# Wide fp32 products of TensorE made as four quarter-width products side by side, in a cross-attention kernel

## The chip, the cores and the metric

The kernel runs on one core of a Trainium2 chip. The metric is the device time of one execution in microseconds (us). The core's engines run side by side, each with a queue of its own: TensorE (PE in the profile, its weight loads PEld) multiplies, VectorE (DVE) and ScalarE (ACT) do elementwise work and reductions, GpSimd (POOL) does some of that too, and SyncE (SP) issues the transfers between the core's memory and HBM.

## The reference

A cross-attention layer with a second, "adapter" attention, all in fp32, over x of 2 batches, 2048 rows and 640 columns, and a context of 2 x 128 rows and 384 columns. The last 4 context rows (`ca`) feed the adapter, the other 124 (`enc`) the text attention:

```python
query = hidden_states @ Wq
keyt = enc @ Wk
valt = enc @ Wv
hs = _mha(query, keyt, valt)                     # 8 heads of 80 columns
ca_q1 = jnp.einsum('btc,th->bch', ca, Wq_ca)[:, indices, :]
ca_hs1 = _mha(ca_q1, residual, residual)         # 2048 x 2048, with 384 distinct rows
ca_q2 = ca_hs1 @ Wq
ca_hs2 = _mha(ca_q2, ca @ Wk_ca, ca @ Wv_ca)
out = (hs + ca_hs2) @ Wout + b_out
out = out + residual
```

## The kernel before, in words

**Products.** A product has a stationary operand `lhsT` (rows x columns), loaded into TensorE as weights, and a moving operand `rhs` with the same rows; the result has as many partitions as `lhsT` has columns. Every fp32 product gives two weight loads and two matmul records in the trace. A product of 128 rows by 128 columns fills TensorE's array ("wide" below). Smaller ones fill a part of it, and several that lie in different parts stand side by side: the profile writes `128*32` for 128 rows by 32 columns (a "strip"), `64*128` and `32*128` for products that fill some of the rows. The wide ones are the query projection (`pq`, from x turned, `xt`, and Wq; for six of the eight blocks of 512 rows in a form with fewer products and sums of x and Wq, `queries_fast`), the output projection (`po`, from the hidden states `hs` and Wout, also with sums; and `po2` with `w2_sb`), and in the setup `pk`, `pv`, `pw`, `pa`. Products that were already strips are `ph` (`hidden`: probabilities `pT` by the values `vpad`, 16 units of 24 products) and `acc` (`contract`: the adapter's `ea` by `y_sb`). The text scores `sc` are 64 rows high, the adapter's scores `s` 32 rows, `pyz` 64 rows. Transposes (`pt_...`, `pm`) and the idle products on zeros at the start (`idle_work`, tile `unread`) take the whole array.

**Work.** x comes in by eight blocks of 512 rows (`x_load`), each turned by DVE. For each block TensorE makes the queries and `pyz`. The adapter (`adapter`) takes `s` twice per batch: once for the maxima (DVE reduces, tile `mx`), once for the exponentials (ACT, tile `ea`), which `contract` multiplies into `acc`; `second` ends it. The text attention goes by 16 units of 256 rows: scores `sc`, softmax over DVE, ACT and POOL, the probabilities out to HBM and back in another order (`kept`, `pT`), `ph`, then four chains of `po`, each added to the residual rows by DVE and stored.

**Order.** The program is written out by a planner, `Desk`. Every operation is a `Do` with an engine, what it waits for, the rooms (PSUM banks, buffers) that it takes, a rank, and for some of TensorE's a `mode`, the shape that it needs of the array. `run` takes the operation that can start first by the planner's own estimate of time; among those that can start at once on an engine it takes the one with the lowest rank plus `change(mode)`:

```python
WHOLE, SWITCH, LEAVE, ANOTHER = (P, P), 12.6, 12.9, -0.8
def change(self, mode):
    if mode is None or mode == self.mode:
        return 0.0
    return self.LEAVE if self.mode == self.WHOLE else self.SWITCH if mode == self.WHOLE else self.ANOTHER
```

So an operation pays 12.9 for leaving the favoured shape, 12.6 for entering it, -0.8 between others. Modes are given for `pq` and `po` ((128, 128)), `ph` ((128, 32)) and `sc` ((64, 128)); `acc`, `s`, `pyz` and transposes have none. Ranks: queries 10 + 2n for block n, `sc` m (10 + m once no query slot is free), `ph` and `po` 30 + m (60 + m before the adapter's part is there), adapter scores 0, `acc` 0.5. `RANKS` adds a number to the n-th task of a kind. The operations of each engine are pinned to the order that comes out. The estimate has a cost to start in a shape (`START`) and to leave one (`DRAIN`, `DRAINS`), and `2 * n / 1.2` ns for an fp32 product with n moving columns, shared by those that fit side by side.

Line 213 of the profile is the call in `Desk.matmul`, 223 that of `transpose`, 238 that of all engines but TensorE and the queues, 258 that of a transfer.

Of the kernel before, what the change touches and what calls it, by code (L numbers as in the profile page):

```python
# [14 lines left out]
P = 128  # L15
# [49 lines left out]
class Desk:  # L65
# [1 line left out]


    ENGINES = ("PE", "ACT", "DVE", "POOL", "SP", "NONE")
    WHOLE, SWITCH, LEAVE, ANOTHER = (P, P), 12.6, 12.9, -0.8  # L70
    START = {(P, P): 0.107, (64, P): 0.143, (P, 64): 0.107, (64, 32): 0.1, (P, 32): 0.03}
    DRAIN = {
        ((P, P), (32, P)): 0.136, ((P, P), (64, P)): 0.035, ((P, P), (P, 64)): 0.056, ((P, P), (P, 32)): 0.067,
# [136 lines left out]
        self.mode, self.idle = mode, False  # L210

    def matmul(self, out, lhsT, rhs, **kw):
        self.pin(self.nc.tensor.matmul(out, lhsT, rhs, **kw))  # L213
        n = 1
        for size in rhs.shape[1:]:
            n *= size
        self._mode(*lhsT.shape)
        at_once = (P // self.mode[0]) * (P // self.mode[1])
        one = lhsT.dtype == F32R
        self.spent += self.slow() * (1 if one else 2) * max(n / 1.2, 107) / 1e3 / at_once  # L220

    def transpose(self, out, in_, ident):
        self.pin(self.nc.tensor.transpose(out, in_, ident))
# [41 lines left out]
def kernel(  # L265
# [40 lines left out]
    desk = Desk(tc)  # L306
    matmul, transpose, copy, dma = desk.matmul, desk.transpose, desk.copy, desk.dma
# [7 lines left out]
    banks, xslots, qslots, rows, staging = Room(4), Room(2), Room(3), Room(0), Room(1)  # L315
# [57 lines left out]
    wq4 = const.tile([P, NCH, P], F32, name="wq4")  # L373
# [150 lines left out]
    def idle_work():  # L524

        zeros = sp.tile([P, P], F32, name="zeros")
        yield Do("DVE", lambda: desk.v_memset(zeros, 0.0), [])

        op = yield Do("NONE", lambda at: (bank(at[0], "unread"), at[0]), needs=[(banks, 1)])
        to, at = op.value
        for n in range(IDLE):

            def product():
                matmul(to[:, :P], zeros, zeros, start=True, stop=True)

            yield Do("PE", product, [] if n else [op.at], frees=[(banks, at)] if n == IDLE - 1 else [])

# [559 lines left out]
    def queries(n, after, first=False):  # L1099

        b, sb = divmod(n, NSB)
        yield Do("NONE", lambda: None, after)
        t, at = xt[b, sb]

        def room(s):
            q_of[n] = q_slot(s[0], f"q_{n}"), s[0]

        if first:
            yield Do("NONE", room, after, needs=[(qslots, 1)])
            q = q_of[n][0]  # L1110
            op = yield Do("NONE", lambda s: [bank(i, f"pq_{n}_{c}") for c, i in enumerate(s)], [], needs=[(banks, 3)])
            pq, three = op.value, op.slots[0]
            for i in range(NCH):

                def part(i=i):
                    for c in range(3):
                        matmul(
                            pq[c], wq_of(i, c), t[:, :, i, :], start=(i == 0), stop=(i == NCH - 1)
                        )

                op = yield Do("PE", part, [*after, ("wq", i)])
            for c in range(3):
                yield Fork(one(evacuate(q[:, c, :], pq[c], three[c], after=[op.at], marks=[("qc", n, c)])), 4)
        for c in range(3 if first else 0, NCH):

            def part(s, z=None, c=c):
                if z:
                    room(z)
                pq = bank(s[0], f"pq_{n}_{c}")
                for i in range(2):  # L1130
                    matmul(pq, wq_of(i, c), t[:, :, i, :], start=(i == 0), stop=False)
                return pq

            own = [(qslots, 1)] if n not in q_of else []
            op = yield Do("PE", part, [*after, "wq4"], needs=[(banks, 1), *own], mode=(P, P))
            pq, s, q = op.value, op.slots[0][0], q_of[n][0]

            for i0, i1 in ((2, 4), (4, NCH)):

                def part(c=c, i0=i0, i1=i1):  # L1140
                    for i in range(i0, i1):
                        matmul(pq, wq_of(i, c), t[:, :, i, :], start=False, stop=(i == NCH - 1))

                op = yield Do("PE", part, mode=(P, P))
            if c < 4:
                yield Fork(one(evacuate(q[:, c, :], pq, s, after=[op.at], marks=[("qc", n, c)], rank=0)), 0)
            else:
                yield Fork(halves_away(n, pq, s, op.at) if n else first_halves(pq, s, op.at), 0)
        used(b, sb, op)
        yield Do("NONE", lambda: None, [("qc", n, c) for c in range(4)], marks=[("q", n)])  # L1150
# [49 lines left out]
    def queries_fast(n, after):  # L1200
# [16 lines left out]
        rank = 10 + 2 * n  # L1217
# [14 lines left out]
        def chain(c, steps):  # L1232

            po, s, at = None, None, []
            for k, ((x, y, plus), ready, (i, u)) in enumerate(steps):

                def product(s=None, z=None, k=k, x=x, y=y):
                    if z:
                        q_of[n] = q_slot(z[0], f"q_{n}"), z[0]
                    to = bank(s[0], f"pq_{n}_{c}") if s else po  # L1240
                    for m in range(2):
                        for j in range(2):
                            matmul(
                                to[:, m * 2 * P : (m + 1) * 2 * P], x[:, j, m], y[:, :, j, :],
                                start=(k == 0 and m == 0 and j == 0), stop=(j == 1), skip_group_check=True,
                            )
                    return to

                def fifth(i=i, u=u):
                    for m in range(2):  # L1250
                        matmul(
                            po[:, m * 2 * P : (m + 1) * 2 * P], wq_of(4, 2 * i + m),
                            t[:, 2 * u : 2 * u + 2, 4, :], start=False, stop=True, skip_group_check=True,
                        )

                if x is not None:
                    needs = ([(banks, 1)] if k == 0 else []) + ([(qslots, 1)] if n not in q_of else [])
                    op = yield Do("PE", product, ready + at, needs=needs, mode=(P, P))
                    if k == 0:
                        po, s = op.value, op.slots[0][0]  # L1260
                    if n not in forked:
                        forked.add(n)
                        desk.event(("q slot", n)).t = desk.now
                        for c2 in (1, 2, 3):
                            yield Fork(chain(c2, chains[c2]), rank + 0.1 * c2)
                if plus:
                    op = yield Do("PE", fifth, [op.at] + at, mode=(P, P))
                counted(op, any(key[0] == "xs" for key in ready))
                yield from read(i, u, po, s, op.at, k == len(steps) - 1)
                at = [desk.event(("qr", n, i, u, len(begun_of[n, i, u]) - 1))]  # L1270
# [28 lines left out]
    def plain(n, t, c, rank, counted):  # L1299

        def part(s):
            pq = bank(s[0], f"pq_{n}_{c}")
            for i in range(2):
                matmul(pq, wq_of(i, c), t[:, :, i, :], start=(i == 0), stop=False)
            return pq

        op = yield Do("PE", part, needs=[(banks, 1)], mode=(P, P), rank=rank)
        pq, s = op.value, op.slots[0][0]
        for i0, i1 in ((2, 4), (4, NCH)):

            def part(i0=i0, i1=i1):
                for i in range(i0, i1):
                    matmul(pq, wq_of(i, c), t[:, :, i, :], start=False, stop=(i == NCH - 1))

            op = yield Do("PE", part, mode=(P, P), rank=rank)
        counted(op, False)
        yield Fork(halves_away(n, pq, s, op.at), 0)

# [726 lines left out]
    def text_out_fast(m, rank):  # L2045
# [3 lines left out]
        for c0, n in ((0, 2), (2, 2), (4, 1)):  # L2049

            def product(s, z=None, c0=c0, n=n):
# [4 lines left out]
            op = yield Do(  # L2056
                "PE", product, [("pT", m), "v done"], needs=[(banks, 1)] + ([(hss, 1)] if c0 == 0 else []),
                frees=[(pTs, room_of["pT", m])] if c0 == 4 else [],
                mode=(P, 32), rank=rank,
            )  # L2060
            (hs, fifth), at_hs = fast_of[m]
            to = hs[:, c0 : c0 + n].rearrange("p c t -> p (c t)") if c0 < 4 else fifth
# [28 lines left out]
        ready = [("xr", m)]  # L2091
# [8 lines left out]
        def chain(n, steps):  # L2100

            po, s, at = None, None, []
            for k, ((x, y, plus), after, ((i, u),)) in enumerate(steps):

                def product(s=None, k=k, x=x, y=y, plus=plus):
# [9 lines left out]
                    return to  # L2115

                op = yield Do(
                    "PE", product, after + at + ready, needs=[(banks, 1)] if k == 0 else [], mode=(P, P), rank=rank
                )
                if k == 0:  # L2120
                    po, s = op.value, op.slots[0][0]
# [10 lines left out]
                op = yield Do("DVE", add, [op.at], frees=[(banks, s)] if end else [], rank=1)  # L2132
                at = [op.at]
# [76 lines left out]
    for n, (b, sb) in enumerate(blocks):  # L2210
        if n:
            after = [("x", *blocks[n - 1])] + ([("q", n - NSB + 1)] if n >= NSB else [])
# [40 lines left out]
```

## Time and profile before

| what | us |
|---|---|
| median of 3 runs | 602.38 |
| lowest and highest of them | 601.35, 602.93 |
| span of the profiled execution, first to last instruction | 600.3 |
| TensorE busy in it (97%) | 583.0 |
| VectorE busy (67%) | 404.1 |
| ScalarE busy (47%) | 282.2 |
| GpSimd busy (25%) | 151.1 |

The span leaves out what lies before the first and behind the last instruction; the median stands 2.1 us above it. The profile gives every instruction's start; the starts of matmuls are recorded, their ends are modelled (they are pipelined, so one record's length overlaps the next one's start). What a group of matmuls takes is therefore read from the start of its first record to the start of the next group.

### The profile page before, as it was taken

The page shows a single profiled execution, that of the slowest core. Times are in us where ns is not written, and L with a number is a line of the kernel's source. Part 1 is how long each engine was busy: PE and PEld are TensorE (multiplying, and loading weights), DVE is VectorE, ACT ScalarE, POOL GpSimd, SP SyncE. Part 2 cuts the span into 40 slices and gives each one's busy share as a digit, 9 for nine tenths or more (in the row PEclk, how much of TensorE's full clock was granted, in tenths as well). Part 3 has the DMA queues.
Part 4 walks back from the last instruction along what each step waited for, and adds up shares of the span by engine and source line. Part 5 has one row for each costly group of instructions (what it writes and reads, how often), then busy time and mean ns, then how long its engine had stood idle before and what let it go on. Part 6 is the DMA issues. An engine that isn't in the chain of part 4 may idle for free.

```text
span 600.3 us, 11804 instructions
## 1 busy us (share of the span) xinstructions
PE 583.0 (97%) x4535; PEld 363.2 (61%) x4535; DVE 404.1 (67%) x640; ACT 282.2 (47%) x770; POOL 151.1 (25%) x201
## 2 busy tenths in 40 slices
PE   9999989999999999999999999999999999999997
PEld 7575455756757655465666555666555557676664
DVE  2257698989999977464999999996422153344343
ACT  2233156455445499799844443345765741201010
POOL 7201021413215330004104443133112202062251
PEclk9999999999999999999999999999999999999999
DMA  8998825965969495454796999786943495799995
GB/s 278 176 238 161 153 80 166 178 178 172 137 170 212 136 184 179 150 161 141 189 265 193 258 216 277 227 218 183 241 128 79 101 255 125 231 217 285 231 236 160
DMA packets 152818, 113.55 MB, mean 189 GB/s; under 512 B 83253, under 2 KB 125621, under 8 KB 152762
## 3 DMA queue, kind: packets, MB, share of 16 engines
q1 hardware_dynamic: 147130, 102.11, 66.2%
q0 software_dynamic: 5632, 10.69, 10.2%
q8 instruction: 36, 0.59, 0.4%
q14 instruction: 20, 0.16, 0.1%
HBM read 71.89 MB, written 40.88 MB: 188 GB/s over the span
## 4 chain that ended last, share of the span: by engine, by line
PE 61%; DVE 23%; DMA 6%; ACT 6%; issue 3%; SPq 0%; DVEq 0%; ACTq 0%
PE po L213 23%; PE pq L213 11%; DVE mx L238 8%; PE acc L213 6%; PE ph L213 6%; DMA pT<-kept 5%; PE s L213 4%; DVE m L238 3%; ACT p L238 3%; PE sc L213 2%; ACT ea L238 2%; DVE eb L238 2%; PE pyz L213 2%; DVE q L238 2%; DVE zop L238 1%
## 5 line engine op out<-in xcount | busy, mean ns | idle before, releaser
L238 DVE TENSOR_REDUCE mx<-s 128x4 f32<-128x2048 f32 x48 | 109.2, 2276 | 6.2 <-PE s L213 6.2
L238 ACT ACTIVATE p<-sc,m 128x124 f32<-128x124 f32 x256 | 90.6, 385 | 31.3 <-DVE m L238 31.2
L238 ACT ACTIVATE ea<-s 128x2048 f32<-128x2048 f32 x48 | 91.3, 1903 | 26.9 <-PE s L213 26.8
L213 PE MATMUL pq<-xt,wq_sb 128*128 128x256 f32 (+1 forms) x272 | 86.1, 452 | 2.4 <-DVE q L238 2.3
L238 POOL TENSOR_TENSOR p<-p,r 128x992 f32<-128x992 f32 x19 | 35.5, 1869 | 203.7 <-DVE r L238 203.7
L213 PE MATMUL po<-wout_sums,hs 128*128 128x320 f32 x256 | 78.8, 440 | 0.0
L213 PE MATMUL po<-wout_sb,hs 128*128 128x320 f32 x240 | 75.0, 442 | 1.6 <-ACT p L238 1.3
L238 DVE TENSOR_TENSOR x_more<-x_more,po 128x320 f32<-128x320 f32 x72 | 34.3, 482 | 47.4 <-PE po L213 44.4
L213 PEld LDWEIGHTS pq<-xt,wq_sb 128*128 128x128 f32 x272 | 48.8, 190 | 27.0 <-issue 17.0
L213 PEld LDWEIGHTS po<-wout_sums,hs 128*128 128x128 f32 x256 | 46.7, 190 | 23.0 <-issue 5.4
L213 PEld LDWEIGHTS po<-wout_sb,hs 128*128 128x128 f32 x240 | 43.6, 189 | 25.9 <-issue 6.1
L238 DVE TENSOR_TENSOR last_rows<-last_rows,po 128x320 f32<-128x320 f32 x56 | 27.2, 486 | 46.0 <-PE po L213 45.6
L238 ACT ACTIVATION_READ_ACCUMULATOR p<-sc,m 128x1 f32 x256 | 58.0, 227 | 0.0
L238 ACT COPY hs<-ph 128x512 f32<-128x512 f32 (+1 forms) x34 | 18.5, 560 | 78.1 <-PE ph L213 78.1
L213 PE MATMUL acc<-ea,y_sb 128*32 128x384 f32 (+2 forms) x768 | 51.4, 385 | 0.0
L2003 POOL DMA_INDIRECT x_more<-o,query x18 | 28.1, 1560 | 91.7 <-DVE x_more L238 80.6
L238 DVE TENSOR_REDUCE m<-sc 128x4 f32<-128x496 f32 x64 | 40.3, 662 | 10.8 <-PE sc L213 10.8
L213 PE MATMUL ph<-pT,vpad 128*32 128x256 f32 x768 | 45.6, 381 | 1.2 <-DMA pT<-kept 1.0
L238 DVE STREAM_TRANSPOSE eb<-p 128x1024 f32<-128x1024 f32 x32 | 39.4, 1232 | 1.9 <-DMA kept<-eb 1.7
L213 PE MATMUL pq<-xt,wq 128*128 128x512 f32 x80 | 39.8, 612 | 0.0
L213 PEld LDWEIGHTS sc<-kmain,q 64*128 64x128 f32 x512 | 31.1, 187 | 12.8 <-issue 6.3
L213 PE MATMUL sc<-kmain,q 64*128 64x124 f32 x512 | 37.1, 284 | 0.0
(207 smaller groups left out, 787.1 us busy)
## 6 DMA issues: line engine op xcount, KB each, us to landing
kept<-eb SPq DMA_DIRECT2D x32, 512.0 KB
pT<-kept SPq DMA_DIRECT2D x64, 256.0 KB
landing<-away SPq DMA_DIRECT2D x60, 128.0 KB
xi<-in_x_dram SPq DMA_DIRECT2D x28, 256.0 KB
x_more<-in_x_dram SPq DMA_DIRECT2D x18, 320.0 KB
out_dram<-x_more SPq DMA_DIRECT2D x18, 320.0 KB
last_rows<-in_x_dram SPq DMA_DIRECT2D x14, 320.0 KB
out_dram<-last_rows SPq DMA_DIRECT2D x14, 320.0 KB
```

The lines of the kernel that those rows point to most:

```text
L213: self.pin(self.nc.tensor.matmul(out, lhsT, rhs, **kw))
L238: self.pin(getattr(engine, what)(*args, **kw))
L2003: desk.pin(nc.gpsimd.indirect_dma_start(out=t, out_offset=None, in_=o2_of[b], in_offset=bass.IndirectOffsetOnAxis(ap=query[:, st : st + 1] ...
```

## The change

`Desk.matmul` splits a product with more than 64 rows and more than 64 columns into four of 32 columns. Each takes 32 columns of the weights, all of the moving operand, and writes 32 partitions of the result. The planner's favoured shape becomes (128, 32), the modes of `pq` and `po` too, and the idle products at the start get a call of their own that keeps them whole. `RANKS`, the surcharges and the tables of starts and drains stay.

```diff
-    WHOLE, SWITCH, LEAVE, ANOTHER = (P, P), 12.6, 12.9, -0.8
+    WHOLE, SWITCH, LEAVE, ANOTHER = (P, 32), 12.6, 12.9, -0.8
...
     def matmul(self, out, lhsT, rhs, **kw):
-        self.pin(self.nc.tensor.matmul(out, lhsT, rhs, **kw))
+
+        rows, cols = lhsT.shape
+        wide = rows > 64 and cols > 64
+        for c in range(0, cols, 32) if wide else (0,):
+            strip = slice(c, c + 32 if wide else cols)
+            self.pin(self.nc.tensor.matmul(out[strip], lhsT[:, strip], rhs, **kw))
         n = 1
         for size in rhs.shape[1:]:
             n *= size
-        self._mode(*lhsT.shape)
+        self._mode(rows, 32 if wide else cols)
         at_once = (P // self.mode[0]) * (P // self.mode[1])
         one = lhsT.dtype == F32R
-        self.spent += self.slow() * (1 if one else 2) * max(n / 1.2, 107) / 1e3 / at_once
+        self.spent += self.slow() * (1 if one else 2) * max(n / 1.2, 107) / 1e3 / at_once * (4 if wide else 1)
+
+    def warm(self, out, zeros):
+        self.pin(self.nc.tensor.matmul(out, zeros, zeros, start=True, stop=True))
+        self._mode(P, P)
+        self.spent += self.slow() * 0.214
...
-                matmul(to[:, :P], zeros, zeros, start=True, stop=True)
+                desk.warm(to[:, :P], zeros)
...
-            op = yield Do("PE", part, [*after, "wq4"], needs=[(banks, 1), *own], mode=(P, P))
+            op = yield Do("PE", part, [*after, "wq4"], needs=[(banks, 1), *own], mode=(P, 32))
...
-                    "PE", product, after + at + ready, needs=[(banks, 1)] if k == 0 else [], mode=(P, P), rank=rank
+                    "PE", product, after + at + ready, needs=[(banks, 1)] if k == 0 else [], mode=(P, 32), rank=rank
```

The other five such lines of the diff make the same change of `mode` in `queries`, `queries_fast` and `plain`.

More of the change, by code (lines that the diff above doesn't have):

```diff
@@ L1142, in part @@
                         matmul(pq, wq_of(i, c), t[:, :, i, :], start=False, stop=(i == NCH - 1))
-                op = yield Do("PE", part, mode=(P, P))
+                op = yield Do("PE", part, mode=(P, 32))
             if c < 4:
@@ L1257, in chain @@
                     needs = ([(banks, 1)] if k == 0 else []) + ([(qslots, 1)] if n not in q_of else [])
-                    op = yield Do("PE", product, ready + at, needs=needs, mode=(P, P))
+                    op = yield Do("PE", product, ready + at, needs=needs, mode=(P, 32))
                     if k == 0:
@@ L1266, in chain @@
                 if plus:
-                    op = yield Do("PE", fifth, [op.at] + at, mode=(P, P))
+                    op = yield Do("PE", fifth, [op.at] + at, mode=(P, 32))
                 counted(op, any(key[0] == "xs" for key in ready))
@@ L1305, in part @@
             return pq
-        op = yield Do("PE", part, needs=[(banks, 1)], mode=(P, P), rank=rank)
+        op = yield Do("PE", part, needs=[(banks, 1)], mode=(P, 32), rank=rank)
         pq, s = op.value, op.slots[0][0]
@@ L1313, in part @@
                     matmul(pq, wq_of(i, c), t[:, :, i, :], start=False, stop=(i == NCH - 1))
-            op = yield Do("PE", part, mode=(P, P), rank=rank)
+            op = yield Do("PE", part, mode=(P, 32), rank=rank)
         counted(op, False)
```

## The prediction, made before the changed kernel was run

> **What bounds the kernel now.** I read the page's first lines, then busy time by stretch, then the matmul groups by shape, then the timeline of TensorE (PE) for the joints between groups.
>
> ```profile
> span 600.3 us, 11804 instructions
> PE 583.0 (97%) x4535; PEld 363.2 (61%) x4535; DVE 404.1 (67%) x640; ACT 282.2 (47%) x770; POOL 151.1 (25%) x201
> ```
> ```profile
> 0.00:75.00 75.00, 73.87 (x397) 43.50 (x398) 36.39 (x95) 19.52 (x47) 19.23 (x92) 1.00 0.93 201
> 75.00:140.00 65.00, 63.31 (x393) 40.54 (x392) 58.93 (x83) 36.51 (x141) 15.51 (x12) 1.00 0.63 156
> 140.00:220.00 80.00, 76.41 (x558) 51.99 (x556) 78.87 (x104) 42.48 (x153) 29.62 (x31) 1.00 0.75 167
> 220.00:290.00 70.00, 68.46 (x791) 39.58 (x787) 40.99 (x64) 64.47 (x138) 6.10 (x6) 1.00 0.52 151
> 290.00:390.00 100.00, 95.32 (x740) 60.45 (x731) 97.38 (x116) 45.41 (x182) 28.83 (x22) 1.00 0.92 239
> 390.00:495.00 105.00, 104.44 (x1076) 59.32 (x1076) 48.72 (x92) 61.77 (x89) 23.96 (x20) 1.00 0.69 172
> 495.00:596.00 101.00, 101.00 (x603) 67.80 (x601) 42.15 (x90) 12.04 (x25) 27.89 (x18) 1.00 0.88 217
> ```
>
> The columns are stretch, its length, busy time (and instructions) of PE, weight loads, DVE, ACT, POOL, then the granted clock and DMA. PE is full nearly everywhere and its clock is 1.00. But in 140 to 220 and 290 to 390 DVE is as full as PE (78.87 of 80 us, 97.38 of 100), so PE time saved there may become PE waiting; 75 to 140 (58.93 of 65) leans the same way. In 220 to 290 and from 390 on, DVE has room and a saved PE microsecond is a saved microsecond.
>
> The products that the change touches, 128 rows by 128 columns, two records each:
>
> ```profile
> L213 PE MATMUL po<-wout_sums,hs 128*128 128x320 f32 x256 | 78.8, 440 | 0.0
> L213 PE MATMUL po<-wout_sb,hs 128*128 128x320 f32 x240 | 75.0, 442 | 1.6 <-ACT p L238 1.3 <-DVE hs L238 0.2
> L213 PE MATMUL po<-wout_sb,wout_sums 128*128 128x320 f32 x80 | 27.4, 435 | 0.0
> L213 PE MATMUL pq<-xt,wq_sb 128*128 128x256 f32 x192 | 48.9, 392 | 2.4 <-DVE q L238 2.3
> L213 PE MATMUL pq<-x_sums,wq_sb 128*128 128x256 f32 x96 | 23.7, 390 | 2.5 <-DVE q L238 2.3
> L213 PE MATMUL pq<-x_sums,wq_sums 128*128 128x256 f32 x96 | 23.0, 382 | 0.0
> L213 PE MATMUL pq<-xt,wq 128*128 128x512 f32 x80 | 39.8, 612 | 0.0
> L213 PE MATMUL pq<-xt,wq_sb 128*128 128x512 f32 x80 | 37.2, 597 | 0.0
> ```
>
> That is 576 records of 320 columns, 384 of 256 and 160 of 512: 1120 together (smaller rows add a few; I leave them out of the sum). Now the joints, from the timeline (start, length, group):
>
> ```profile
> 570.33 2.80 PE L213 MATMUL ph<-pT,vpad 128*32 128x256 f32 x48
> 573.06 1.34 PE L213 MATMUL po<-wout_sb,hs 128*128 128x320 f32 x4
> 574.24 2.32 PE L213 MATMUL po<-wout_sums,hs 128*128 128x320 f32 x8
> ...
> 590.62 4.47 PE L213 MATMUL po<-wout_sums,hs 128*128 128x320 f32 x16
> 594.93 1.24 PE L213 MATMUL po<-wout_sb,wout_sums 128*128 128x320 f32 x4
> ```
> ```profile
> 477.56 1.07 PE L213 MATMUL acc<-ea,y_sb 128*32 128x128 f32 x16
> 478.45 1.91 PE L213 MATMUL ph<-pT,vpad 128*32 128x256 f32 x32
> 480.29 0.51 PE L213 MATMUL s<-cop,zop 32*128 32x256 f32 x8
> ...
> 481.73 1.34 PE L213 MATMUL po<-wout_sb,hs 128*128 128x320 f32 x4
> 483.00 0.56 PE L213 MATMUL s<-cop,zop 32*128 32x128 f32 x8
> ```
>
> **Pace.** A wide record of 320 columns takes (594.93 - 590.62)/16 = 0.269 us; in proportion, 256 columns take 0.2155. The kernel already makes products of 128 rows by 32 columns, `ph` and `acc`, four side by side. The 32 `ph` records from 478.45 (behind `acc`, same shape) take 1.84 us to the next group: 8 groups of four at 0.2155 are 1.72, and 0.116 is left for leaving the shape. The 48 from 570.33 take 2.73: 12 groups are 2.59, leaving is 0.116, and 0.028 is left for entering. So four strips go through in the time of one wide product. The bound on the other side: if entering were free, the two rows give 0.89 us per four groups, 0.2225 each, 3% over the wide pace. Quarter-width products then cost 0 to 3% in pace; I take 0, since entering is not free for the wide shape either.
>
> **Joints.** Wide: 573.06 to 574.24 is 1.18 us for 4 records of 0.269, so entering costs 0.10 (rounded rows; I use 0.104); 481.73 to 483.00 is 1.27, which leaves 0.09 for leaving (0.094). For strips: enter 0.028 (I use 0.025), leave 0.115. Between two groups of one shape, nothing.
>
> **The change part by part.** (a) The arithmetic: each of the 1120 records becomes four that run side by side, at the pace above: 0. PE gets 3360 more records (4535 to about 7,900, weight loads too), one every 76 ns on average instead of 132. Whether PE can be fed at that rate is a rival below. If the pace is the 3% bound instead, 576 x 0.269 + 384 x 0.2155 + 160 x 0.431 = 307 us grow by 9, and that stays in the range.
>
> (b) The joints. I walked PE's timeline and counted changes of shape, if the order stays. For each kind stand the rows that begin after its first and its last place:
>
> ```profile
> 38.99 0.38 PE L213 MATMUL pa<-first_rows,blk_k 128*128 128x128 f32 x1
> ...
> 586.21 1.07 PE L213 MATMUL po<-wout_sb,hs 128*128 128x320 f32 x3
> ```
> ```profile
> 23.63 1.02 PE L213 MATMUL p_kca<-w_kca,cadT 128*32 128x160 f32 x24
> ...
> 583.48 2.80 PE L213 MATMUL ph<-pT,vpad 128*32 128x256 f32 x48
> ```
> ```profile
> 57.43 1.88 PE L213 MATMUL pv<-w_v,ctxT 128*128 128x320 f32 x6
> ...
> 451.50 0.81 PE L213 MATMUL po<-wout_sums,hs 128*128 128x320 f32 x2
> ```
> ```profile
> 9.89 2.84 PE L213 MATMUL pq<-xt,wq_sb 128*128 128x512 f32 x6
> 12.57 0.38 PE L223 MATMUL pt_ctx<-ident,ctx_sb 128*128 128x128 f32 x2
> ...
> 495.33 0.49 PE L223 MATMUL pt_p<-ident,p2pad 128*113 128x128 f32 x3
> 495.66 0.70 PE L213 MATMUL po<-wout_sums,hs 128*128 128x320 f32 x2
> ```
>
> Strips to wide, 47 places: one shape from now on, saves 0.115 + 0.104 each: -10.3 us. Wide to strips, 9 places: saves 0.094 + 0.025: -1.1. Rows (32 or 64 high: `s`, `sc`, `pyz`) to wide, 57 places: entering falls from 0.104 to 0.025: -4.5. Wide to rows, 96 places, the last the `s` at 483.00 above: leaving rises from 0.094 to 0.115: +2.0. Transposes and the idle products stay 128 wide: into them 17 places, now leave 0.115 plus entering, which no row separates; between 0 (no dearer than any next record) and 0.104 (a wide product), I take 0.08, the nearer shape's price a little cut as transposes are short: +3.3; out of them 19 places, 0.094 + 0.025: +2.3. Sum -8.3 us.
>
> (c) Where it lands: +1.9 in 0 to 75 (most transposes), -1.5 in 75 to 220, -2.4 in 220 to 290, -1.7 in 290 to 390, -4.6 after. Of the -3.2 in the stretches that DVE fills I count a third, because DVE is late next there: -8.3 + 2.1 = -6.2.
>
> (d) The order. PE's order is drawn up by the planner with a surcharge on changing shape (12.9 to leave the favoured shape, 12.6 to enter it). The favoured shape is now the strip, so `ph` and `acc` lie inside it: after an `acc` group `po` and `pq` cost nothing extra and `sc` costs 12.9. The order from 220 us on will differ, and no row prices it. Bounds: PE's idle time in 75 to 390 is 1.69 + 3.59 + 1.54 + 4.68 = 11.5 us by the windows; all of it gone is -11.5, as much again is +11.5. Before 220 there are hardly any strips, so little changes. I take 0, midway, as the surcharges still hold the groups together.
>
> No wait is added. A group's last strip starts about 0.02 us after its first, which is in the 0.115.
>
> **Sum**: 600.3 - 6.2 = 594.1 of span. The median of the runs, 602.4, stands 2.1 over this span; on its scale I forecast **596.2**. Its own range: DVE takes all (-5.1) or nothing (-8.3) and entering a transpose costs 0 to 0.104, together 592.7 to 597.7.
>
> A rule that speaks against this: the Trainium skill, page "TensorE: Matmul & The Clock Gate", section "Measured speedup vs the span model", measures three column strips at 2.38 times one, not 3. Its own model there, one product plus about 4 ns per tile, would give full pace; the 0.02 us between first and last strip agrees with the model.
>
> **Rivals.**
>
> *The new order starves DVE (slower).* Place: 290 to 390, where DVE is at 97% and everything that follows needs its results. If `sc` is put off behind `po` and `pq` by its 12.9, the softmax, the turn and `ph` behind it come later, and PE waits. For it: strips are now inside the favoured shape, so `sc` pays nearly always. Against: `sc` outranks `po` of its unit by 20 to 30, more than 12.9. Price: the idle time doubles, +11.5: 607.7. It decides against the change once idle time grows by over 6.2 us. The mirror case, idle time shrinking by most of itself, gives 587.
>
> *PE cannot be fed (slower).* Four 256-column strips need a record every 54 ns and a weight load with it.
>
> ```profile
> 472.04:480.26 8.22, 8.22 (x152) 4.42 (x144) 1.78 (x5) 7.40 (x8) 2.32 (x4) 1.00 0.57 138
> 470.70:490.70 20.00, 20.00 (x295) 10.68 (x295) 6.43 (x15) 14.23 (x15) 4.08 (x6) 1.00 0.84 202
> ```
>
> The densest stretches shown are 54 ns a record over 8 us and 68 over 20. If 68 were the limit, a 256 group would take 0.272 for 0.2155 (384 x 0.056 = 21.7 us) and a 320 group 0.272 for 0.269 (1.7): 596.2 + 23.4 = 619.6. Against it: nothing in those rows idles, and `pq` bursts are short between `s` groups. I put 0 in the sum. The same page (section "Wait — 56ns, not 53.3ns?") states about 62 ns of sequencer work per matmul in one decoding mode; by that figure a 256 group would take 0.248, about +12 us. No run here shows which mode holds.
>
> *Strips do not run four abreast here.* In `ph` and `acc` neighbouring strips read different data or pairs of it; now all four read the same. If that let only two run at a time, a group would take twice the wide time, and the 307 us of pace would double: 903. The `ph` rows, where two strips share their data at full pace, speak against it. By the skill's 2.38 for three, the 307 us would grow by a factor of 1.26, to about 676.
>
> **How the numbers follow.** Joints saved, order neutral: 0.50. Idle time shrinks: 0.09. Order gives back all or more: 0.30, of which 0.12 within 0.3% of before (1.8 us, about what a measurement here can tell from no change). PE unfed: 0.08. Strips not abreast: 0.03. So faster 0.59, same 0.12, slower 0.29. The range, 588 to 611, holds the forecast and most of both orders, and leaves out the last two.
>
> **What would show it.** About 7,900 PE records; `po` groups of four every 0.27 us and `pq` ones every 0.216, also late in long bursts (else unfed, or not abreast); no gap where `ph` or `acc` meets `po`; `s` to `po` 0.08 shorter; PE's idle time in 75 to 390 near 11.5 us. I am wrong if the idle time grows by more than the joints give, or if DVE-filled stretches keep their length and PE idles in them by all that was saved.

## The result and the profile after

The changed kernel takes 625.6 us (median of 4 runs, 624.8 to 626.3) against 602.65 for the kernel before: the ratio is 1.0373, 95% interval 1.0338 to 1.0409. The forecast was 596.2, the range 588 to 611; the chance of slower was 0.29.

First the page of the changed kernel (line 213 is now 218, 223 is 233, 238 is 248, 258 is 268), then the same stretches as before: length, busy time and instructions of PE, weight loads, DVE, ACT, POOL, granted clock, DMA.

```profile
span 624.6 us, 19410 instructions
PE 583.8 (93%) x8321; PEld 292.1 (47%) x8321; DVE 406.6 (65%) x645; ACT 278.6 (45%) x762; POOL 152.4 (24%) x204
```
```profile
0.00:75.00 75.00, 70.86 (x811) 32.83 (x811) 36.75 (x96) 17.77 (x42) 18.98 (x92) 1.00 0.85 191
75.00:140.00 65.00, 60.20 (x800) 29.71 (x796) 53.08 (x71) 29.68 (x119) 11.96 (x10) 0.97 0.58 142
140.00:220.00 80.00, 74.26 (x1106) 40.36 (x1094) 75.84 (x101) 39.16 (x149) 22.17 (x20) 0.98 0.68 165
220.00:290.00 70.00, 67.50 (x1021) 33.92 (x1019) 41.66 (x70) 62.41 (x137) 10.74 (x15) 1.00 0.59 153
290.00:390.00 100.00, 93.72 (x1370) 48.20 (x1370) 89.30 (x111) 47.58 (x168) 31.43 (x26) 0.98 0.86 232
390.00:495.00 105.00, 103.00 (x1565) 51.81 (x1569) 65.30 (x99) 56.42 (x116) 27.99 (x23) 1.00 0.81 199
495.00:624.00 129.00, 114.20 (x1682) 55.32 (x1671) 44.68 (x101) 25.61 (x36) 29.15 (x21) 0.96 0.78 199
```

PE is busy for as long as before (583.8 against 583.0 us). All of the loss is idle time: 624.6 - 583.8 = 40.8 us against 600.3 - 583.0 = 17.3. From 75 to 390 it is 4.8 + 5.7 + 2.5 + 6.3 = 19.3 us, where it was 11.5. Much of that growth is in the waits of the adapter's scores `s` for DVE's maxima, here first after and then before (total us, times, longest):

```profile
PE s L218 <- DVE mx L248: 8.1, 6, 2.1
```
```profile
PE s L213 <- DVE mx L238: 0.5, 1, 0.5
```

The largest growth, 11.3 us of the 23.5, lies behind 495: to the end of the span PE is idle for 15.4 us, 3.7 of them behind its last product; before it was 4.1, all behind the last product. There the timeline of PE reads (start, length, group, idle time before it and its releaser):

```profile
585.70 1.26 PE L218 MATMUL po<-wout_sums,hs 128*32 128x320 f32 x16
592.20 2.29 PE L218 MATMUL po<-wout_sums,hs 128*32 128x320 f32 x16 [5.24 <-DVE x_more L248]
594.24 2.54 PE L218 MATMUL po<-wout_sb,hs 128*32 128x320 f32 x24
599.54 2.36 PE L218 MATMUL po<-wout_sums,hs 128*32 128x320 f32 x16 [2.75 <-DVE last_rows L248]
```

and the chain that ended last, at its end, shows what DVE itself was waiting for:

```profile
544.84 8.08 PE po L218 x120
555.15 6.98 DMA last_rows<-o,query
562.18 6.57 DMA out_dram<-last_rows
568.77 6.56 DMA last_rows<-early
576.05 9.37 DMA last_rows<-o,query
585.43 5.29 DMA out_dram<-last_rows
591.16 9.67 DMA out_dram<-x_more
600.85 3.84 DMA x_more<-in_x_dram
609.11 6.06 DMA last_rows<-o,query
```

Before, the chain's last 100 us were `po` and `ph`; it ended

```profile
573.13 10.43 PE po L213 x38
583.55 2.73 PE ph L213 x48
586.28 9.90 PE po L213 x36
```

Now the last 70 us are mostly row buffers that are stored, loaded and added to one after the other. The adapter is late: its last transposes (`pt_p`) stand at

```profile
521.72 0.55 PE L233 MATMUL pt_p<-ident,p2pad 128*113 128x128 f32 x3 [0.67 <-DVE p2pad L248]
```

against 495.33 before. Tiles whose `po` is done before the adapter's result is there go out to HBM as `early`, come back and get their rows added: seven tiles here,

```profile
early<-last_rows SPq DMA_DIRECT2D x4, 320.0 KB, 3.1
early<-x_more SPq DMA_DIRECT2D x3, 320.0 KB, 4.7
```

two in the kernel before:

```profile
early<-last_rows SPq DMA_DIRECT2D x1, 320.0 KB
early<-x_more SPq DMA_DIRECT2D x1, 320.0 KB
```

So the trace says that the pieces, where the clock was full, were not slower but stood in another order. Whether strips themselves had a share in it had to be tried.

### The profile page after: what moved, and what is told of

The parts are those of the page before. It is cut to its first block, busy times and chain, and to the rows that moved or that the text cites. A ratio compares the mean times of both kernels' runs of the same rounds, so it can differ in the third digit from the quotient of the medians.

```text
span 624.6 us, 19410 instructions
## 1 busy us (share of the span) xinstructions
PE 583.8 (93%) x8321; PEld 292.1 (47%) x8321; DVE 406.6 (65%) x645; ACT 278.6 (45%) x762; POOL 152.4 (24%) x204
## 4 chain that ended last, share of the span: by engine, by line
PE 60%; DVE 16%; DMA 12%; ACT 5%; issue 3%; SPq 2%; POOL 0%; POOLq 0%; ACTq 0%; DVEq 0%
PE po L218 19%; PE pq L218 16%; PE acc L218 5%; PE s L218 5%; DVE mx L248 4%; PE ph L218 4%; PE sc L218 4%; DMA last_rows<-o,query 4%; ACT p L248 2%; ACT ea L248 2%; SPq L268 2%; DMA out_dram<-last_rows 2%; DMA out_dram<-x_more 2%; DVE m L248 2%; DVE eb L248 1%
## 5 line engine op out<-in xcount | busy, mean ns | idle before, releaser
L218 PE MATMUL po<-wout_sums,hs 128*32 128x320 f32 x1024 | 82.5, 451 | 11.1 <-DVE x_more L248 5.9
L218 PE MATMUL pq<-xt,wq_sb 128*32 128x256 f32 (+1 forms) x1088 | 86.3, 450 | 0.0
L218 PE MATMUL po<-wout_sb,hs 128*32 128x320 f32 x992 | 78.0, 439 | 0.7 <-DVE hs L248 0.5
L248 DVE TENSOR_TENSOR last_rows<-last_rows,po 128x320 f32<-128x320 f32 x56 | 26.8, 484 | 50.6 <-PE po L218 40.8
L2013 POOL DMA_INDIRECT x_more<-o,query x21 | 32.8, 1561 | 96.1 <-DVE x_more L248 66.6
L218 PEld LDWEIGHTS po<-wout_sums,hs 128*32 128x32 f32 x1024 | 32.4, 112 | 47.0 <-issue 8.5
L218 PE MATMUL ph<-pT,vpad 128*32 128x256 f32 x768 | 49.0, 385 | 3.4 <-ACT p L248 3.4
L218 PEld LDWEIGHTS pq<-xt,wq_sb 128*32 128x32 f32 x1088 | 32.6, 111 | 37.6 <-issue 23.6
L218 PEld LDWEIGHTS po<-wout_sb,hs 128*32 128x32 f32 x992 | 31.7, 112 | 35.2 <-issue 4.5
L218 PE MATMUL sc<-kmain,q 64*128 64x124 f32 x512 | 38.4, 287 | 2.2 <-DVE q L248 1.4
L218 PE MATMUL pq<-xt,wq 128*32 128x512 f32 x320 | 38.8, 596 | 0.5 <-DVE q L248 0.4
```

The lines of the kernel that those rows point to most:

```text
L218: self.pin(self.nc.tensor.matmul(out[strip], lhsT[:, strip], rhs, **kw))
L248: self.pin(getattr(engine, what)(*args, **kw))
L2013: desk.pin(nc.gpsimd.indirect_dma_start(out=t, out_offset=None, in_=o2_of[b], in_offset=bass.IndirectOffsetOnAxis(ap=query[:, st : st + 1] ...
```

## The experiments

**Order and strips taken apart.** The change does two things: it emits strips, and it makes the planner reckon with strips. Each was run alone. The first kernel emits strips; the planner's lines stay as before, and with them the order of every engine. (Line numbers in the profile shift by some lines from kernel to kernel.)

```diff
+        rows, cols = lhsT.shape
+        wide = rows > 64 and cols > 64
+        for c in range(0, cols, 32) if wide else (0,):
+            strip = slice(c, c + 32 if wide else cols)
+            self.pin(self.nc.tensor.matmul(out[strip], lhsT[:, strip], rhs, **kw))
...
         self._mode(*lhsT.shape)
```

> The wide products are emitted as four strips, but the planner reckons with them as before (favoured shape, modes, estimates), so every engine's order is that of the kernel before. Theory A (the strips are as good as predicted, the new order lost the time): the joints are saved, 594 to 599 us, PE's idle time near the 13 us of before plus a few us where DVE is full. Rival B (strips themselves cost, by feeding or contention): 612 us or more, with late records inside long bursts. Rival C (half and half): 603 to 611 us.

Measured: 600.4 us, ratio 0.9968 (0.9950 to 0.9986). Its page:

```profile
span 598.6 us, 19382 instructions
PE 575.6 (96%) x8321; PEld 289.6 (48%) x8321; DVE 402.6 (67%) x640; ACT 282.0 (47%) x770; POOL 151.4 (25%) x201
```

PE's busy time falls by 7.4 us, but idle time grows by 5.7, from 17.3 to 23.0, so 1.7 us of span are left. Rival B is out, and theory A holds for the strips, not for what was to come of them: they make a kernel that is faster by 0.3%, short of the 594 to 599 us.

The second takes the changed kernel and emits every wide product whole, the planner reckoning as if they were strips.

```diff
-        for c in range(0, cols, 32) if wide else (0,):
-            strip = slice(c, c + 32 if wide else cols)
-            self.pin(self.nc.tensor.matmul(out[strip], lhsT[:, strip], rhs, **kw))
+        self.pin(self.nc.tensor.matmul(out, lhsT, rhs, **kw))
```

> The planner reckons as in the changed kernel, so the order is that of the changed kernel, but every wide product is emitted whole. Theory A: the changed kernel's 625.6 us plus the joints that strips had saved, 628 to 636 us, with the adapter as late as there (its last transposes near 522 us, 495 before). Rival B: near the kernel before, 600 to 606 us.

Measured: 632.25 us, ratio 1.0474 (1.0423 to 1.0525). The order alone costs 30 us, and in that order strips are the better by 6.7 us (632.25 - 625.6, two sessions whose medians of the kernel before differ by 0.7). Both are as theory A had it, and the adapter is late here too: its last transposes stand at 525.54.

**Why the new order is bad.** The planner adds a number from `RANKS` to the n-th task of a kind. If the table fits one run of the plan only, the change spoils it without being at fault. It was emptied (`RANKS = {}`) in both kernels, which ran once each.

> The kernel before with its table of extra ranks (RANKS) emptied. Theory A1 (the table is fitted to one order and is worth much there): 615 to 635 us. Rival A2 (the table is worth little, and the surcharges inside the planner's rule make the new order worse): 600 to 610 us.

> The changed kernel with RANKS emptied. Theory A1: the table no longer fits there, so without it the time is 610 to 630 us, no worse than the changed kernel by more than a few us, and below the kernel before without the table by the saved joints. Rival A2: the new surcharges are at fault, so it stays 15 us or more above the kernel before without the table.

Measured: 620.4 us for the kernel before without its table, 608.35 for the changed one without it. The same table is worth 18 us to the one and costs the other 17. Without it the changed kernel is the faster one by 12 us, so the new surcharges as such do no harm, and rival A2 falls as far as one execution each can tell. Theory A1 was off in size for the second: 608.35 lies below its 610 to 630, and 12 us are more than the saved joints.

How closely the table fits was tried in the kernel before, with wide products whole and one estimate moved by 3 ns:

```diff
-    START = {(P, P): 0.107, (64, P): 0.143, (P, 64): 0.107, (64, 32): 0.1, (P, 32): 0.03}
+    START = {(P, P): 0.110, (64, P): 0.143, (P, 64): 0.107, (64, 32): 0.1, (P, 32): 0.03}
```

> The kernel before, wide products whole, with one number of the planner's table changed: the estimated start of a wide product 0.110 us instead of 0.107. Theory A1 (the table of extra ranks is fitted so closely that any change of the estimates spoils it, so the change's loss needs no property of strips): 608 to 618 us. Rival A2 (only a change of the surcharges, such as the favoured shape, makes a bad order): within 2 us of the kernel before.

Measured: 613.4 us, ratio 1.0184 (1.0139 to 1.0230). Three nanoseconds in a table of the planner cost 12 us of time on the chip. Theory A1 holds for this one estimate; others were not tried. Here too `s` waits for the maxima (10.7 us in all; 8.1 in the changed kernel, 0.5 before), but the last transposes of the adapter stand at 501.21, and PE does not wait for row buffers at the end. So a spoilt table costs in part in other places each time, and which of the change's lines in the planner spoilt it was not taken apart.

**Where the joints of the old order went.** Strips in the old order saved 7.4 us of PE and won 1.7. They reached the first adapter scores at 55.67 us against 52.60 (the expectation below names both half a microsecond later). 1.35 of these 3 us are a wait in the setup that the kernel before does not have:

```profile
46.32 0.33 PE L232 MATMUL pt_a<-ident,a 128*128 128x128 f32 x1 [1.35 <-DVE kmain L247]
```

To see whether the 3 us were the rest of the gain, products that the planner places before 47 us stayed whole (the cut is against the kernel with strips in the old order):

```diff
-        wide = rows > 64 and cols > 64
+        wide = rows > 64 and cols > 64 and self.now > 47
```

> As the strips in the old order, but products that the planner places before 47 us stay whole, so that setup's transposes and wide products share a shape again. If the 3 us by which strips in the old order were late at the first adapter scores (56.2 against 53.2 us) come from joints between transposes and strips, and are carried to the end: 597 to 598.5 us. If DVE and the other waits further on swallow them: 600 to 601 us, like strips in the old order.

Measured: 599.8 us (597.5 to 604.0), ratio 0.9969 (0.9942 to 0.9997). That lies between the two bands, and the ratio is the same as with strips in the setup. The first scores do come early now, at 51.63 us; but 0.8 of the 1.0 us against the kernel before stands there already at `p_kca` (22.87 against 23.63), where the two kernels hold the same instructions. Rows of ACT and PE in this kernel show what took the lead back:

```profile
77.26 1.02 ACT L247 CAST krest<-k_parts 128x992 fp32r<-128x992 f32 x1 [2.98 <-DMA k_parts<-k_away]
```
```profile
80.49 1.90 PE L217 MATMUL pq<-xt,wq 128*32 128x512 f32 x16
86.04 1.93 PE L217 MATMUL pq<-xt,wq_sb 128*32 128x256 f32 x32 [3.65 <-DVE q L247]
```

Before, the same cast ran without a wait, and PE's wait at that place was 1.59 us:

```profile
75.86 1.02 ACT L238 CAST krest<-k_parts 128x992 fp32r<-128x992 f32 x1
```
```profile
84.63 1.99 PE L213 MATMUL pq<-xt,wq_sb 128*128 128x256 f32 x8 [1.59 <-DVE q L238]
```

The rest of the keys lands at 77.3 us although everything else stands ready earlier; ACT waits 3.0 us for it and PE, behind DVE, 3.65. The gain at the start is hidden behind a transfer. With strips in the setup too, where PE is later, the cast did not wait:

```profile
78.21 1.02 ACT L247 CAST krest<-k_parts 128x992 fp32r<-128x992 f32 x1
```

**A table of its own for the changed kernel.** If only the fit is lost, a new fit should bring the joints out. The changed kernel got a table found by changing one to three numbers at a time and keeping what brought the planner's reckoned end forward.

> The changed kernel with a table of extra ranks fitted anew to it (by the planner's own reckoning of the end, which it brings from 616.7 to 590.0 us; it reckons 600.9 for the kernel before). Theory A1 (the loss is only a misfit of the table): below both kernels, 590 to 598 us. Rival A2 (strips or the favoured strip shape hold the kernel back in some way that the planner does not reckon with): 600 us or more.

The same order with whole products tells the strips' share, the kernel before with its own table fitted further tells what a fit alone gives. The edits are the table (197 numbers, some 60 for `chain`), and for the second the emission as above.

> The order of the refitted kernel, with every wide product emitted whole. If strips save their joints in this order too: 5 to 9 us above the refitted strips. If the gain of the refit is all order: the same as the refitted strips within 2 us.

> The kernel before with its own table fitted further in the same way and for as long (by the planner's reckoning from 600.9 to 598.7 us), wide products whole. Theory A1: its table was near its best, so 598 to 602 us, and the strips with a table of their own are lower by 3 to 9 us. Rival: the further fit is worth as much as the strips, 592 to 596 us.

Measured: 597.9 us for the refitted strips, ratio 0.9898 (0.9867 to 0.9929), faster than both kernels by their ratios, at the upper edge of the band; 605.4 us for the same order with whole products, ratio 1.0025 (1.0005 to 1.0044); 610.6 us for the further fit of the kernel before, ratio 1.0124 (1.0090 to 1.0159). Refitted strips first, the same order whole below:

```profile
span 596.9 us, 19433 instructions
PE 573.1 (96%) x8321; PEld 299.6 (50%) x8321; DVE 402.9 (68%) x651; ACT 277.0 (46%) x756; POOL 156.2 (26%) x204
```
```profile
span 605.1 us, 11853 instructions
PE 587.9 (97%) x4535; PEld 361.3 (60%) x4535; DVE 405.0 (67%) x651; ACT 277.1 (46%) x756; POOL 156.4 (26%) x204
```

In this order strips take 14.8 us off PE's busy time and 7.5 off the medians. With whole products the order is no better than that of the kernel before; the win is the strips', in an order that suits them. On the timelines, wide products and strips meet in 92 places of this order (56 from strips to wide, 36 back), in the order of the kernel before in 56 (47 and 9), and there strips won 0.3%. The refitted kernel sends out six tiles as `early`, nearly as many as the changed one, but its last transposes stand at 491.83: `early` tiles as such do not cost the time.

The last run missed both its bands: the planner reckoned its further fit 2.2 us better and it came out 1.2% slower. The planner's reckoning fell short of the measured medians by 1 us (600.9 for the kernel before) up to 12 (598.7 for the last run), so it can tell tens of microseconds and not two.

## Why the prediction was wrong, point by point

**Pace: right.** Four strips go through in the time of one wide product, also where all four read the same data. In the changed kernel

```profile
578.81 1.26 PE L218 MATMUL po<-wout_sums,hs 128*32 128x320 f32 x16
579.88 1.26 PE L218 MATMUL po<-wout_sb,hs 128*32 128x320 f32 x16
580.96 1.26 PE L218 MATMUL po<-wout_sb,wout_sums 128*32 128x320 f32 x16
582.04 2.77 PE L218 MATMUL ph<-pT,vpad 128*32 128x256 f32 x48
```

16 records, four groups, take 1.07 to 1.08 us: 0.269 a group, the wide record's time. The bound of 3% was not needed, and "strips do not run four abreast" falls. By the Trainium skill's 2.38 for three column strips ("TensorE: Matmul & The Clock Gate", section "Measured speedup vs the span model") a group would have taken 0.34 us, an estimate.

**Feed: right at 0.** PE got 8321 records; the prediction's 7,900 left the smaller wide products out. The stretch of the changed kernel

```profile
278.70:298.70 20.00, 20.00 (x352) 11.87 (x352) 11.47 (x18) 18.00 (x37) 1.74 (x3) 1.00 0.50 145
```

has a record every 57 ns with a weight load each, for 20 us, PE full. In it, 32 `pq` strips of 256 columns take 1.84 us (from 283.38 to 285.22), 54 ns a record once leaving the shape is taken off, just as the `ph` strips did. The 68 ns that priced this rival was the mean of a stretch in which PE was full too, but in part with whole products. The 62 ns per matmul that the Trainium skill gives for one decoding mode ("TensorE: Matmul & The Clock Gate", section "Wait — 56ns, not 53.3ns?") did not bind here.

**Joints: right in size.** In the old order PE's busy time fell by 7.4 us where the sum had 8.3. Between strips of different products nothing is lost: in the rows above, `ph` follows `po` at 582.04 after the same 1.08 us that lie between two `po` groups. The rows

```profile
479.08 1.07 PE L217 MATMUL acc<-ea,y_sb 128*32 128x384 f32 x16
479.97 1.26 PE L217 MATMUL po<-wout_sb,hs 128*32 128x320 f32 x16
481.19 0.56 PE L217 MATMUL s<-cop,zop 32*128 32x128 f32 x8
```

(strips in the old order) are 2.11 us from `acc` to `s`; the same three groups before took 2.27, and the prediction's prices give 0.20 for the difference of 0.16.

The prices hold in the other two orders as well. With changes of shape counted on the timelines of the kernels with whole products, they give 12.9 us for the new order and 15.2 for the refitted one. PE's busy time differs by 14.4 there (598.2 against 583.8, of which some 2.5 us is the clock of the last section, so 11.9 are left) and by 14.8.

**Where they land, step (c): too small a loss, and elsewhere.** I gave 2.1 of the 8.3 us up to stretches that DVE fills. In the old order 5.7 us went into idle time, and only 1.5 of them lie in those stretches (75 to 220 and 290 to 390). 1.3 lie in 0 to 75, all of it the wait for `kmain`; 1.5 in 220 to 290, where I had counted a saved microsecond as a saved microsecond, and where `s` waits for ACT's `ea` (2.8 us over the run, 1.4 before); 0.4 from 390 to 495; 1.0 behind 495, at the end. I had looked at DVE's share alone; a wait needs no engine that is full, only one that is later than PE now is.

**The order, step (d): this step failed.** Its own sign of being wrong came: idle time grew by 23.5 us, more than the joints give. I took 0 and bounded it by doubling the 11.5 us of idle time between 75 and 390, "as the surcharges still hold the groups together". The runs show 30 us for the order with whole products (632.25 against 601.9) and 25 with strips (625.6 against 600.4). Two things were wrong. I held the order to change where strips are, from 220 us on, by the rule that changed; but the estimates feed the same sort, a 3 ns change of one does as much as 12 us, and PE's order departs from the old one at 24.6 us. And I held idle time to the stretches where there was some; nearly half of the new idle time is at the end, where PE had none before its last product. The chain reads there as if the late adapter had turned `po` into a queue for row buffers; no run made the adapter early with the rest of this order kept, so that last link is read and not tested. Idle time was not all either: the whole loss against strips in the old order is 26.0 us of span, 17.8 of idle time and 8.2 of PE being busy longer, which the last section accounts for.

**The rival "the new order starves DVE"** had the right sign and half the price. DVE does come later (`s` waits 8.1 us for its maxima, 0.5 before), but the rival's place was wrong: 290 to 390 lost only 1.6 us more than before. Against its reason, `sc` put off by its 12.9, speaks that without the table the new surcharges give the faster kernel.

## What to carry to other kernels

When a planner draws up the order from estimates, a change to an operation is also a change to the order of everything else: run the new operation in the old order, and the old operation in the new order, before judging either. A table of hand-fitted ranks belongs to one plan; measure without it what the change is worth, and refit before comparing. Time saved on a full engine counts only up to the next thing that lands late, and that can be a transfer which nobody waited for.

## What the runs showed of the hardware

The clock can fall behind short waits. In the changed kernel, after 5.24 and 2.75 us of idle PE,

```profile
592.20:595.60 3.40, 3.40 (x28) 1.46 (x32) 0.00 (x0) 0.00 (x0) 1.54 (x1) 0.52 1.08 227
599.50:603.00 3.50, 3.46 (x32) 1.58 (x36) 0.78 (x2) 0.00 (x0) 0.00 (x0) 0.56 1.02 271
```

the granted clock is 0.52 and 0.56 for about 3.4 us, and the 16 `po` records from 592.20 take 2.04 us instead of 1.08. There are six such stretches (from about 121, 196, 333, 592, 599 and 616 us), each of 3.4 to 3.8 us at 0.51 to 0.56, and the last waits ahead of them were 1.83, 2.05, 3.05, 5.24, 2.75 and 2.37 us. The length of the wait alone does not decide: in the kernel whose setup products stay whole, the clock stayed at 1.00 behind 3.65 us before 86.04. What else decides stays open.

Over the whole run the mean clock is 0.982, before it was 1.00; so the idle time costs more than itself. PE is busy 8.2 us longer here than with strips in the old order (583.8 against 575.6). Its busy time times the share of the clock that was not granted, added up microsecond by microsecond, is about 9.8 us (an estimate; 0 with strips in the old order), which is enough for all of the 8.2. More joints have no part in it: the two kernels change between strips and rows about as often, 226 and 230 times. The Trainium skill, "TensorE: Matmul & The Clock Gate", section "What's actually happening", has half rate after an idle window of about 3.4 us; the wait of 5.24 us agrees, but 1.83 to 3.05 us were enough in five places, and 3.65 us were not in the other kernel.
